# Slot numbers loaded from ScalarE's queue, the combined matrix in two tiles, and a finer-cut end, in a LoRA-and-experts kernel

## The chip, the cores and the metric

The kernel runs on one core of a Trainium2 chip. The metric is the device time of one execution in microseconds (us). Five engines matter: TensorE (PE, with its weight loads PEld), VectorE (DVE), ScalarE (ACT), GpSimd (POOL), and SyncE (SP), which only issues transfers. ScalarE and GpSimd can issue transfers as well. Sixteen DMA engines carry them all.

## The reference

Two layers, of which the first is never stored. With x of shape 8 x 512 x 2048:

```
base  = x @ W.T + b
lora  = (x @ A[slot]) @ B[slot] * 2          # slot: one number per batch, rank 16
y     = base + lora
logit = y @ route_w.T                        # 8 experts; the best one wins
h     = y @ Aexp.T                           # 8 x 16 values per token
wh    = h masked to the winning expert, times its logit
out   = x + wh @ Bexp                        # 128 x 2048
```

All arithmetic is float32. Since only logits and h are needed of y, the kernel multiplies W by the projection first: c = W.T @ [Aexp, route_w].T is a matrix of 2048 x 136, and each token then needs x @ c.

## The kernel before

**Fold (lines 352 to 386).** W comes in 16 blocks `w_0` to `w_15` of 1 MB, in four buffers, over SP's queue; the projection `pj` comes in parts, the first two over ScalarE's queue (lines 106 and 130). `chunk_w(oc)` copies a block into a regrouped form `wv`, half on ACT and half on DVE, one block ahead, and then issues the load of block oc + 4. `fold_w(oc)` does 16 matmuls per block into six PSUM tiles `pcs` (pool `ps_c`, one bank each, three chunks of c to a bank, the last bank one). After block 15 each bank is copied into `cm` (line 307), by ACT and DVE in turn. `cm` is one tile of 128 x 16 x 168: per chunk 16 columns of A for even batches, the 136 of c, and 16 columns of A for odd batches. Matmuls, copies and transfers run in the order in which they are written, on each engine; nothing is rescheduled.

**Slot numbers.** `it_i` (line 92) is the 8 slot numbers, copied from one row of DRAM into all 128 partitions by a transfer that GpSimd issues. They are used from line 165 on, for the rows of the adapter gathers.

**Turns in the fold.** The pool `ps_s` (two banks) holds short-lived results: the warm-up, the transposed adapter rows, the projected bias and adapters, and later the transposed heads `pw`.

**Steps (lines 536 to 577).** There are 32 tiles of 128 tokens and two steps per tile. A step n does, on PE, half of the `heads` of tile t (x turned, times `cm`, into a bank `ph`), `add_low` (the low-rank part), `turn_heads` (transposes `wh`), and a half of the `delta` of an earlier tile (`wh` times the experts' B, into two banks `po` of the pool `ps_o`). On DVE it does `route` (five small operations from the best logit to `wh`), `add_delta` (x plus delta, 1024 columns at once) and the turning of x. ACT and POOL regroup x ahead (`shuffle`). `ps_h` (two banks) holds `ph`; `ps_h` and `ps_o` are opened after `ps_c` is closed and take its banks. Once per batch GpSimd puts the A columns of the batch after into `cm` (line 569).

**The end.** Tile 31 is treated apart: its delta goes into single banks, `pe_h` twice in the first half, then `pe_o` (512 columns), `pe_o` (256) and `pe_s` (256); each is added and stored on its own, every second one over ScalarE's queue. Tile 30 is added and stored by halves of 1024 columns, all earlier tiles are stored whole, over SP's queue.

Of the kernel before, what the change touches and what calls it, by code (L numbers as in the profile page):

```python
# [9 lines left out]
F32 = mybir.dt.float32  # L10
# [8 lines left out]
def kernel(  # L19
# [29 lines left out]
    nc = tc.nc  # L49
    P = 128  # L50
    Q = 32
    NQ = P // Q
    B, T, D = x.shape
# [4 lines left out]
    R = ER // E  # L58
    NJ = D // P
# [3 lines left out]
    NT = B * TPB  # L63
# [4 lines left out]
    HN = D // 512 // 2  # L68
    NA = NP + R
    assert B * R == P and ER == P and DO == D and B == 2 * NQ  # L70

    const = ctx.enter_context(tc.tile_pool(name="const", bufs=1))
# [7 lines left out]
    ps_s = ctx.enter_context(tc.tile_pool(name="ps_s", bufs=2, space=bass.MemoryType.PSUM))  # L80
# [8 lines left out]


    it_i = const.tile([P, B], I32, name="it_i")
    nc.gpsimd.dma_start(out=it_i, in_=itok.to_broadcast([P, B]))
    pj = wpool.tile([P, NO, NP], F32, name="pj")
    proj_v = proj.rearrange("(c p) e -> p c e", p=P)

    def load_pj(c0, c1, eng=nc.sync):
        eng.dma_start(out=pj[:, c0:c1, :], in_=proj_v[:, c0:c1, :])
# [30 lines left out]

    nc.scalar.copy(warm_a[:, 1:2], warm_a[:, :1])
    load_pj(1, 3, nc.scalar)  # L130
    pm = ps_s.tile([P, P], F32, tag="s", name="pm")
    for _ in range(14):
        nc.tensor.matmul(pm, warm, warm, start=True, stop=True)
# [93 lines left out]

    cm = const.tile([P, NJ, NA + R], F32, name="cm")  # L230
    ad_aT = const.tile([P, NJ, P], F32, name="ad_aT")
    ad_bT = tpool.tile([P, NJ, P], F32, tag="t", name="ad_bT")
    g4 = const.tile([P, B, NP], F32, name="g4")
# [58 lines left out]
    def fold_w(oc):  # L292
        for q, (pc, (j0, n)) in enumerate(zip(pcs, groups)):
            for k in range(n):

                h, j = divmod(j0 + k, HJ)
                nc.tensor.matmul(  # L297
                    pc[:, k, :],
                    wv_tiles[oc, h][:, j, :],
                    pj[:, oc, :],  # L300
                    start=(oc == 0 and k == 0),
                    stop=(oc == NO - 1),
                    skip_group_check=True,
                )
            if oc == NO - 1:
                copy = nc.scalar.copy if q % 2 == 0 else nc.vector.tensor_copy
                copy(cm[:, j0 : j0 + n, R:NA], pc[:, :n, :])  # L307


    bp = wpool.tile([P, NP], F32, name="bp")  # L310
# [42 lines left out]
    for oc in range(NO):  # L353
        if oc + 1 < NO:
            chunk_w(oc + 1)
        fold_w(oc)
        if oc == 2:
            fill_constants()
        if oc == 4:
            load_adapters_b()  # L360
        if oc == 7:
            load_adapters_a()
        if 8 <= oc < 12:
            turn_adapters(oc - 8)
        if oc in (9, 10):
            fold_bias(range(8 * (oc - 9), 8 * (oc - 8)))
        if oc == 8:
            load_x(0)
            shuffle(0, moves[6:], nc.gpsimd.tensor_copy)
        if oc == 11:  # L370
            nc.sync.dma_start(out=fb, in_=ffn_b)
            load_x(1)
            load_x(2)
            project_bias()
        if oc in (10, 11):
            turn(ad_aT, ad_ar, oc - 10)
        if oc == 11:
            for b in range(2):
                nc.vector.tensor_copy(cm[:, :, ds(b * NA, R)], ad_aT[:, :, ts(b, R)])
        if oc == 12:  # L380
            project_adapters()
        if oc in (12, 13, 14):
            shuffle(0, moves[2 * (oc - 12) : 2 * (oc - 11)], nc.scalar.copy)
        if oc == 14:
            for h in range(2):
                turn_x(0, h)
    wctx.close()
    ps_h = ctx.enter_context(tc.tile_pool(name="ps_h", bufs=2, space=bass.MemoryType.PSUM))
    ps_o = ctx.enter_context(tc.tile_pool(name="ps_o", bufs=2, space=bass.MemoryType.PSUM))
# [4 lines left out]
    ph_tiles = {}  # L394
# [4 lines left out]
    po_tiles = {}  # L399

    def batch_of(t):
        return t // TPB

    def heads(t, j0, j1):
        s = batch_of(t) % 2
        if j0 == 0:
            ph_tiles[t] = ps_h.tile([P, 512], F32, tag="h", name=f"ph_{t}")[:, :NA]
        for j in range(j0, j1):
            nc.tensor.matmul(  # L409
                ph_tiles[t],  # L410
                xT_tiles[t][:, j, :],
                cm[:, j, ds(s * R, NA)],
                start=(j == 0),
                stop=(j == NJ - 1),
            )
# [15 lines left out]
    def add_low(t):  # L431
        b = batch_of(t)
        nc.tensor.matmul(  # L433
            ph_tiles[t][:, ds((1 - b % 2) * R, NP)],
            hT_tiles.pop(t),
            g4[:, b, :],
            start=False,
            stop=True,
            skip_group_check=True,
        )  # L440
# [21 lines left out]
    def turn_heads(t):  # L462
        pw = ps_s.tile([P, P], F32, tag="s", name=f"pw_{t}")
        nc.tensor.transpose(pw, wh_tiles.pop(t), ident)  # L464
        pw_tiles[t] = pw

    def keep_heads(t):
        whT_tiles[t] = small.tile([P, P], F32, tag="whT", name=f"whT_{t}")
        nc.scalar.copy(whT_tiles[t], pw_tiles.pop(t))  # L469

    def delta(t, h, within=None):

        c0 = h * D // 2
        if t < NT - 1:
            po = ps_o.tile([P, HN, 512], F32, tag="o", name=f"po_{t}_{h}")
            cuts = [(512, po[:, k, :]) for k in range(HN)]
            adds = [(ds(c0, D // 2), po.rearrange("p n d -> p (n d)"))]
        else:

            def bank(pool, tag, n):  # L480
                shape = [P, HN, 512] if tag == "o" else [P, 512]
                b = pool.tile(shape, F32, tag=tag, name=f"pe_{tag}")
                return n, (b[:, 0, :] if tag == "o" else b)[:, :n]

            if h == 0:
                cuts = [bank(ps_h, "h", 512), bank(ps_h, "h", 512)]
            else:
                cuts = [bank(ps_o, "o", 512), bank(ps_o, "o", 256), bank(ps_s, "s", 256)]
            adds = []
        c = c0  # L490
        for n, part in cuts:
            nc.tensor.matmul(part, whT_tiles[t], fb[:, ds(c, n)], start=True, stop=True)  # L492
            if t == NT - 1:
                adds.append((ds(c, n), part))
            c += n
            if within:
                within()
                within = None
        po_tiles[t, h] = adds

    def add_delta(t, h):
        u, k = divmod(t, TPU)
        for m, (cols, part) in enumerate(po_tiles.pop((t, h))):
            xs = x_tiles[u][:, k, cols]
            nc.vector.tensor_tensor(xs, xs, part, ALU.add)  # L505
            if t == NT - 1:
                store(t, cols, nc.scalar if m % 2 else nc.sync)
        if t == NT - 2:
            store(t, ts(h, D // 2))
        elif t < NT - 2 and h == 1:  # L510
            store(t, ds(0, D))

    def store(t, cols, eng=nc.sync):
        u, k = divmod(t, TPU)
        b, r = divmod(t, TPB)
        eng.dma_start(out=out[b, ts(r, P), cols], in_=x_tiles[u][:, k, cols])

    def piece(n):

        return divmod(n - 3, 2) if 0 <= n - 3 < 2 * NT else (-1, -1)  # L520
# [15 lines left out]
    for n in range(2 * NT + 4):  # L536
        t, h = divmod(n, 2)
        if t < NT:

            heads(t, h * HJ, h * HJ + HJ // 2)  # L540
            if n == 2:
                add_low(0)
            if n == 3:
                turn_heads(0)
            heads(t, h * HJ + HJ // 2, (h + 1) * HJ)
        if h == 0 and 0 < t <= NT:
            route(t - 1)
        tp, hp = piece(n - 1)
        if tp >= 0:
            add_delta(tp, hp)  # L550
        turn_x(t + 1, h)
        if h == 1 and 0 < t <= NT:
            keep_heads(t - 1)
        u, ms = shuffle_slot(n)
        shuffle(u, ms, nc.gpsimd.tensor_copy if n == 2 else nc.scalar.copy)
        if h == 1 and t < NT:
            turn_low(t)
        last = n in (2 * NT - 1, 2 * NT)
        if last:

            delta(*piece(n), (lambda: add_low(t)) if h else (lambda: turn_heads(t - 1)))
        elif piece(n)[0] >= 0:
            delta(*piece(n))
        if h == 1 and 0 < t < NT and not last:
            add_low(t)
        if h == 1 and t < NT:
            b, k = divmod(t, TPB)
            if k == 0 and 0 < b < B - 1:
                nc.gpsimd.tensor_copy(
                    cm[:, :, ds((b + 1) % 2 * NA, R)], ad_aT[:, :, ts(b + 1, R)]  # L570
                )
        if h == 0 and 1 < t <= NT and not last:
            turn_heads(t - 1)
        tq, hq = piece(n - 5)
        u, k = divmod(tq, TPU)
        if tq >= 0 and hq == 1 and k == TPU - 1 and u + XB < NU:
            load_x(u + XB)
# [48 lines left out]
```

## Time and profile before

| | |
|---|---|
| median of 3 runs | 334.77 us (334.49 to 335.0) |
| profiled execution | 334.58 us, its span 332.8 us |
| PE busy | 323.9 us, 97% |
| DVE, ACT, POOL busy | 233.7, 171.0, 136.3 us |
| PE clock | 0.999 of full speed |
| HBM traffic | 54.88 MB read, 33.62 MB written, 266 GB/s |

The span runs from the first to the last recorded instruction; the profiled execution's own time is 1.78 us longer. Times in the text count from the span's start. PE's busy share says that the other engines matter only where PE waits for them, and at the two ends of the span, where no PE work runs. A matmul of float32 shows as two records.

### The profile page before, as it was taken

How to read it: one execution, taken by the hardware profiler on the slowest of the kernel's cores; microseconds unless marked ns; L12 is line 12 of the kernel's file. 1: busy time of each engine (PE TensorE's matmuls, PEld its weight loads, DVE VectorE, ACT ScalarE, POOL GpSimd, SP SyncE). 2: the span in 40 equal slices, each digit the busy share in tenths (PEclk: the TensorE clock that was granted, in tenths of full speed). 3: DMA queues.
4: the chain of work that ended last, by engine and by line, in shares of the span. 5: the costliest groups of instructions: out<-in, count | busy, mean ns of one | idle time of the engine just before them, and what ended most of it. 6: DMA issues, size and time to landing. Idle time of an engine off the chain costs nothing.

```text
span 332.8 us, 5119 instructions
## 1 busy us (share of the span) xinstructions
PE 323.9 (97%) x1968; PEld 260.4 (78%) x1968; DVE 233.7 (70%) x425; ACT 171.0 (51%) x193; POOL 136.3 (41%) x143
## 2 busy tenths in 40 slices
PE   8899999999999999999999999999999999999992
PEld 8899999999777777777777777777777777777751
DVE  1133386476877877887878888888878777877753
ACT  3223236646857548565656575757566576630000
POOL 2001503989781609263535536262809081600000
PEclk9999999999999999999999999999999999999999
DMA  7999999958633394857676675849493949333336
GB/s 218 399 405 418 420 407 424 418 221 306 272 161 142 119 391 147 373 173 331 214 292 251 255 291 214 325 183 366 171 376 161 378 174 392 130 126 128 127 145 234
DMA packets 15800, 88.83 MB, mean 267 GB/s; under 512 B 1680, under 2 KB 4640, under 8 KB 5536
## 3 DMA queue, kind: packets, MB, share of 16 engines
q1 hardware_dynamic: 14544, 85.80, 65.7%
q0 software_dynamic: 528, 2.11, 2.0%
q10 hardware_dynamic: 704, 0.60, 0.6%
q8 instruction: 15, 0.25, 0.3%
q14 instruction: 9, 0.07, 0.1%
HBM read 54.88 MB, written 33.62 MB: 266 GB/s over the span
## 4 chain that ended last, share of the span: by engine, by line
PE 94%; DMA 3%; DVE 0%; ACT 0%; SPq 0%; issue 0%; DVEq 0%
PE ph L409 40%; PE po L492 32%; PE pc L297 17%; DMA w<-in_w_dram 3%; PE ph L433 2%; PE pg L342 1%; PE pw L464 1%; PE pbT L324 1%; PE pe_h L492 1%; ACT wv L286 0%; DVE x L505 0%; PE pe_o L492 0%; SPq L103 0%; DVEq L622 0%; DVE cm L307 0%
## 5 line engine op out<-in xcount | busy, mean ns | idle before, releaser
L254 POOL COPY xq<-x 32x1024 f32<-32x1024 f32 x121 | 126.2, 1043 | 118.2 <-DMA x<-in_x_dram 83.9
L254 ACT COPY xq<-x 32x1024 f32<-32x1024 f32 x135 | 140.9, 1043 | 17.9 <-DMA x<-in_x_dram 11.1
L409 PE MATMUL ph<-cm,xT 128*128 128x152 f32 x1024 | 142.6, 293 | 0.5 <-DVE cm L307 0.5
L409 PEld LDWEIGHTS ph<-cm,xT 128*128 128x128 f32 x1024 | 135.1, 190 | 9.3 <-issue 8.7
L492 PE MATMUL po<-fb,whT 128*128 128x512 f32 x248 | 116.7, 592 | 0.0
L505 DVE TENSOR_TENSOR x<-x,po 128x1024 f32<-128x1024 f32 x62 | 75.0, 1210 | 5.6 <-PE po L492 5.5
L239 DVE STREAM_TRANSPOSE xT<-xq 128x1024 f32<-128x1024 f32 x64 | 78.8, 1235 | 0.1
L492 PEld LDWEIGHTS po<-fb,whT 128*128 128x128 f32 x248 | 43.2, 190 | 29.2 <-issue 28.9
L297 PE MATMUL pc<-pj,wv 128*128 128x136 f32 x512 | 60.7, 279 | 1.5 <-ACT wv L286 1.1
L297 PEld LDWEIGHTS pc<-pj,wv 128*128 128x128 f32 x512 | 59.8, 190 | 1.9 <-ACT wv L286 1.3
L469 ACT COPY whT<-pw 128x128 f32<-128x128 f32 x32 | 8.5, 266 | 88.7 <-PE pw L464 88.7
L286 DVE COPY wv<-w 128x1024 f32<-128x1024 f32 (+1 forms) x17 | 13.5, 799 | 29.9 <-PE pc L297 16.1
L446 DVE TENSOR_REDUCE top<-ph 128x1 f32<-128x8 f32 x32 | 5.3, 167 | 37.5 <-PE ph L433 37.5
L286 ACT COPY wv<-w 128x1024 f32<-128x1024 f32 (+1 forms) x17 | 16.8, 996 | 27.9 <-DMA w<-in_w_dram 20.6
L433 PEld LDWEIGHTS ph<-g,hT 128*128 128x128 f32 x64 | 12.0, 190 | 15.0 <-issue 12.2
L452 DVE TENSOR_SCALAR rw<-rank,win,top 128x8 f32<-128x8 f32 x32 | 15.5, 484 | 1.2
L433 PE MATMUL ph<-g,hT 128*128 128x136 f32 x64 | 12.7, 280 | 0.0
L428 DVE STREAM_TRANSPOSE hT<-hls 128x128 f32<-128x128 f32 x32 | 10.0, 311 | 1.1
L173 POOL DMA_INDIRECT raw<-in_cond_b_dram,brow_i x1 | 1.0, 1032 | 23.6 <-DVE brow_i L172 23.6
L464 PEld LDWEIGHTS pw<-ident,wh 128*128 128x128 f32 x32 | 4.5, 140 | 7.7 <-issue 5.0
L454 DVE TENSOR_TENSOR wh<-ph,rw 128x128 f32<-128x128 f32 x32 | 9.3, 292 | 1.1
L464 PE MATMUL pw<-ident,wh 128*128 128x128 f32 x32 | 8.7, 273 | 0.0
(70 smaller groups left out, 81.1 us busy)
## 6 DMA issues: line engine op xcount, KB each, us to landing
x<-in_x_dram SPq DMA_DIRECT2D x32, 1024.0 KB, 8.9
out_dram<-x SPq DMA_DIRECT2D x30, 1024.0 KB, 4.8
w<-in_w_dram SPq DMA_DIRECT2D x16, 1024.0 KB, 11.8
fb<-in_ffn_b_dram SPq DMA_DIRECT2D x1, 1024.0 KB
out_dram<-x SPq DMA_DIRECT2D x2, 512.0 KB, 2.6
pj<-in_proj_dram SPq DMA_DIRECT2D x2, 272.0 KB, 11.4
out_dram<-x SPq DMA_DIRECT2D x2, 256.0 KB, 3.1
g<-g_dram SPq DMA_DIRECT2D x4, 68.0 KB, 2.5
```

Of the source, the lines that this page charges most:

```text
L239: nc.vector.transpose(dst[:, ts(h, HJ), :].rearrange("p j (g t) -> p g j t", t=Q), src.rearrange("p g (j a) -> p g j a", a=Q)[:, :, ts(h, ...
L254: copy(xq_tiles[u][ts(i, Q), :, g, :], x_tiles[u][ts(g, Q), :, ts(i, DQ)])
L286: copy(dst[:, ts(k, n)], wr[:, ds(h * HJ + k * n, n)])
L297: nc.tensor.matmul(pc[:, k, :], wv_tiles[oc, h][:, j, :], pj[:, oc, :], start=(oc == 0 and k == 0), stop=(oc == NO - 1), skip_group_check= ...
L409: nc.tensor.matmul(ph_tiles[t], xT_tiles[t][:, j, :], cm[:, j, ds(s * R, NA)], start=(j == 0), stop=(j == NJ - 1),)
L428: nc.vector.transpose(hT, h.rearrange("p g s -> p (g s)"))
L433: nc.tensor.matmul(ph_tiles[t][:, ds((1 - b % 2) * R, NP)], hT_tiles.pop(t), g4[:, b, :], start=False, stop=True, skip_group_check=True,)
L452: nc.vector.tensor_scalar(rw, rank, win, top, ALU.is_equal, ALU.mult)
L454: nc.vector.tensor_tensor(wh.rearrange("p (e r) -> p e r", r=R), ph[:, :ER].rearrange("p (e r) -> p e r", r=R), rw.unsqueeze(2).to_broadca ...
L464: nc.tensor.transpose(pw, wh_tiles.pop(t), ident)
L492: nc.tensor.matmul(part, whT_tiles[t], fb[:, ds(c, n)], start=True, stop=True)
L505: nc.vector.tensor_tensor(xs, xs, part, ALU.add)
```

## The change

The diff does the following.

- `it_i` is loaded by ScalarE, after its second part of `pj`, and no longer by GpSimd.
- `cm` becomes two tiles, one for chunks 0 to 11 (four of the six fold banks) and one for chunks 12 to 15. The A columns are placed by one copy per tile (`place_a`).
- `ph` of tile 0 is taken from `ps_s` and not from `ps_h`.
- Tile 30 is cut like tile 31: its delta goes into four single banks (`pe_o`, `pe_o`, `pe_h`, `pe_s`), each added and stored on its own by SP. The first of them is added in the step in which it is computed, ahead of `route(31)`. For tile 31 the banks are `pe_h`, `pe_o`, and then `pe_o` (512), `pe_h` (256), `pe_s` (256).

```
-    nc.gpsimd.dma_start(out=it_i, in_=itok.to_broadcast([P, B]))
...
     load_pj(1, 3, nc.scalar)
+    nc.scalar.dma_start(out=it_i, in_=itok.to_broadcast([P, B]))
...
-    cm = const.tile([P, NJ, NA + R], F32, name="cm")
+    JC = NJ * 3 // 4
+    cms = [const.tile([P, n, NA + R], F32, name=f"cm_{n}") for n in (JC, NJ - JC)]
+
+    def cm(j):
+        return cms[j // JC][:, j % JC, :]
+
+    def place_a(b, copy):
+        for k, part in enumerate(cms):
+            n = part.shape[1]
+            copy(part[:, :, ds(b % 2 * NA, R)], ad_aT[:, ds(k * JC, n), ts(b, R)])
...
-                copy(cm[:, j0 : j0 + n, R:NA], pc[:, :n, :])
+                copy(cms[j0 // JC][:, ds(j0 % JC, n), R:NA], pc[:, :n, :])
...
-                nc.vector.tensor_copy(cm[:, :, ds(b * NA, R)], ad_aT[:, :, ts(b, R)])
+                place_a(b, nc.vector.tensor_copy)
...
-            ph_tiles[t] = ps_h.tile([P, 512], F32, tag="h", name=f"ph_{t}")[:, :NA]
+            pool, tag = (ps_h, "h") if t else (ps_s, "s")
+            ph_tiles[t] = pool.tile([P, 512], F32, tag=tag, name=f"ph_{t}")[:, :NA]
...
-                cm[:, j, ds(s * R, NA)],
+                cm(j)[:, ds(s * R, NA)],
...
+    ends = {
+        (NT - 2, 0): (("o", 512), ("o", 512)),
+        (NT - 2, 1): (("h", 512), ("s", 512)),
+        (NT - 1, 0): (("h", 512), ("o", 512)),
+        (NT - 1, 1): (("o", 512), ("h", 256), ("s", 256)),
+    }
...
-        if t < NT - 1:
+        if (t, h) in ends:
+            cuts = ends[t, h]
+        else:
...
-    def add_delta(t, h):
+    def add_delta(t, h, n=None):
...
+        pieces = po_tiles[t, h]
+        po_tiles[t, h] = pieces[n:] if n else []
+        for m, (cols, part) in enumerate(pieces[:n]):
             xs = x_tiles[u][:, k, cols]
             nc.vector.tensor_tensor(xs, xs, part, ALU.add)
-            if t == NT - 1:
-                store(t, cols, nc.scalar if m % 2 else nc.sync)
-        if t == NT - 2:
-            store(t, ts(h, D // 2))
-        elif t < NT - 2 and h == 1:
-            store(t, ds(0, D))
+            if (t, h) in ends:
+                store(t, cols, nc.scalar if t == NT - 1 and m % 2 else nc.sync)
+            elif h == 1:
+                store(t, ds(0, D))
...
             delta(*piece(n), (lambda: add_low(t)) if h else (lambda: turn_heads(t - 1)))
+            if h == 1:
+                add_delta(*piece(n), 1)
...
-                nc.gpsimd.tensor_copy(
-                    cm[:, :, ds((b + 1) % 2 * NA, R)], ad_aT[:, :, ts(b + 1, R)]
-                )
+                place_a(b + 1, nc.gpsimd.tensor_copy)
```

More of the change, by code (lines that the diff above doesn't have):

```diff
@@ L469, in keep_heads, with bank @@
         nc.scalar.copy(whT_tiles[t], pw_tiles.pop(t))
+    def bank(tag, n):
+        pool, shape = {
+            "h": (ps_h, [P, 512]), "s": (ps_s, [P, 512]), "o": (ps_o, [P, HN, 512])
+        }[tag]
+        b = pool.tile(shape, F32, tag=tag, name=f"pe_{tag}")
+        return n, (b[:, 0, :] if tag == "o" else b)[:, :n]
+    ends = {
[4 more added lines that the diff above has]
+    }
     def delta(t, h, within=None):
         c0 = h * D // 2
-        if t < NT - 1:
+        if (t, h) in ends:
+            cuts = ends[t, h]
+        else:
             po = ps_o.tile([P, HN, 512], F32, tag="o", name=f"po_{t}_{h}")
             cuts = [(512, po[:, k, :]) for k in range(HN)]
[L477 to L489, printed above, removed]
-        c = c0
-        for n, part in cuts:
+            po_tiles[t, h] = [(ds(c0, D // 2), po.rearrange("p n d -> p (n d)"))]
+        c = c0
+        for cut in cuts:
+            if (t, h) in ends:
+                cut = bank(*cut)
+                po_tiles.setdefault((t, h), []).append((ds(c, cut[0]), cut[1]))
+            n, part = cut
             nc.tensor.matmul(part, whT_tiles[t], fb[:, ds(c, n)], start=True, stop=True)
-            if t == NT - 1:
-                adds.append((ds(c, n), part))
             c += n
@@ L498, in delta @@
                 within = None
-        po_tiles[t, h] = adds
-    def add_delta(t, h):
+    def add_delta(t, h, n=None):
         u, k = divmod(t, TPU)
-        for m, (cols, part) in enumerate(po_tiles.pop((t, h))):
+        pieces = po_tiles[t, h]
+        po_tiles[t, h] = pieces[n:] if n else []
+        for m, (cols, part) in enumerate(pieces[:n]):
             xs = x_tiles[u][:, k, cols]
             nc.vector.tensor_tensor(xs, xs, part, ALU.add)
-            if t == NT - 1:
-                store(t, cols, nc.scalar if m % 2 else nc.sync)
-        if t == NT - 2:
-            store(t, ts(h, D // 2))
-        elif t < NT - 2 and h == 1:
-            store(t, ds(0, D))
+            if (t, h) in ends:
+                store(t, cols, nc.scalar if t == NT - 1 and m % 2 else nc.sync)
+            elif h == 1:
+                store(t, ds(0, D))
     def store(t, cols, eng=nc.sync):
```

## The prediction

> **What bounds the kernel now.** The page's chain of work that ended last came first. By engine it reads:
>
> ```profile
> PE 94%; DMA 3%; DVE 0%; ACT 0%; SPq 0%; issue 0%; DVEq 0%
> ```
>
> TensorE (PE) works through the span, so an edit pays where PE waits, or after its last matmul. The list of waits names PE's own (total us, times, longest):
>
> ```profile
> PE pc L297 <- ACT wv L286: 1.1, 1, 1.1
> PE ph L409 <- DVE cm L307: 0.5, 1, 0.5
> ```
>
> The chain asked for in order of time (start, duration) places both:
>
> ```profile
> 1.19 9.11 DMA w<-in_w_dram
> 10.32 1.05 ACT wv L286
> 11.42 29.92 PE pc L297 x256
> ...
> 73.02 0.31 DVE cm L307
> ```
>
> PE ends its first fold at 10.28 and starts the second at 11.42, because w_1 lands only at 10.3. At the end of the fold it stops from 73.0 to 73.47 until the last bank has been copied into cm. Why is w_1 late? Busy time by stretches (length, then PE, PEld, DVE, ACT and POOL busy with counts, PE's clock, DMA share, GB/s):
>
> ```profile
> 4.00:5.00 1.00, 1.00 (x9) 1.00 (x9) 0.00 (x0) 0.00 (x0) 0.00 (x0) 1.00 0.99 411
> 5.00:6.00 1.00, 0.98 (x9) 0.79 (x8) 0.17 (x1) 0.17 (x1) 0.00 (x0) 1.00 2.03 265
> 6.00:7.00 1.00, 0.69 (x6) 0.69 (x7) 0.59 (x2) 0.97 (x2) 0.00 (x0) 1.00 0.12 34
> 8.00:9.00 1.00, 1.00 (x11) 1.00 (x10) 0.00 (x0) 0.00 (x0) 0.00 (x0) 1.00 1.00 411
> ```
>
> Traffic nearly stops between 6 and 7 us although w_1 was issued by 1.6. The DMA queues that started packets between 5.5 and 6.0 (packets, MB, share of 16 engines):
>
> ```profile
> q0 software_dynamic: 16, 0.00, 272.1%
> q1 hardware_dynamic: 4, 0.03, 18.9%
> ```
>
> 272.1% of 16 engines for 0.5 us over 16 packets is 1.36 us each: it_i, one packet per DMA engine. The packet records show 0.16 to 1.75 us for 256 B, while bias_o's 512 B packets of the same queue took 27 ns. So this small transfer holds each engine for about 1.36 us, ahead of w_1.
>
> The end, in order of time:
>
> ```profile
> 321.80 0.29 DVE L454 TENSOR_TENSOR wh<-ph,rw 128x128 f32<-128x128 f32 x1
> 322.14 0.14 PEld L464 LDWEIGHTS pw<-ident,wh 128*128 128x128 f32 x1 [0.48 <-DVE wh L454]
> 322.33 0.27 PE L464 MATMUL pw<-ident,wh 128*128 128x128 f32 x1
> 327.01 0.41 DVE L505 TENSOR_TENSOR x<-x,pe_s 128x256 f32<-128x256 f32 x1
> ```
>
> and the stretches after it:
>
> ```profile
> 323.50:324.00 0.50, 0.50 (x2) 0.19 (x1) 0.50 (x1) 0.00 (x0) 0.00 (x0) 1.00 0.00 0
> 324.00:324.50 0.50, 0.50 (x2) 0.19 (x1) 0.50 (x1) 0.00 (x0) 0.00 (x0) 1.00 0.88 360
> 328.00:329.00 1.00, 0.00 (x0) 0.00 (x0) 0.00 (x0) 0.00 (x0) 0.00 (x0) 1.00 1.06 334
> 330.00:330.50 0.50, 0.00 (x0) 0.00 (x0) 0.00 (x0) 0.00 (x0) 0.00 (x0) 1.00 0.15 23
> ```
>
> The 2 MB of the last two tiles start moving at 324.33 and keep the DMA engines full until 330.57: here bandwidth, not the last add (327.42), sets the end.
>
> **What the Trainium skill says.** "DMA: Bandwidth & Descriptors", section Queues, rings and completion order: each engine takes turns between its queues by whole packets. The trace agrees: during a 1.36 us packet of q0, q1 stands still. Same page, Issuing engines are not separate DMA queues: ScalarE's transfers interleave on the same 16 engines, so the move does not take it_i out of the way by itself. "PSUM — Partial Sum Buffer", Specifications: 8 banks of 512 FP32. Here two are in ps_s and six in ps_c, so the heads' banks lie on the fold's; the wait at 73.0 agrees.
>
> **The change, part by part**, on the clock of the profiled execution (334.58 us, span 332.8, 1.78 around it; the median of the runs, 334.77, is 0.19 above it).
>
> *1. it_i on ScalarE's queue.* POOL loses 0.72 us of issue; ident is needed only at 41, so nothing. ScalarE gains one issue of 0.40 us (its other issues), at about 1.65; its next large copy starts at 5.83. In q10's ring it_i stands behind 24 packets per engine of pj, of which the last ran until 10.5, that is after w_1. So w_1 lands about 1.36 us earlier, at 8.95; its copy (1.05) ends at 10.0, before PE is free at 10.28. Gain 11.42 - 10.28 = 1.14, less 0.02: **1.12**. It must survive: chunk 4 (copy at 21.42, ready 22.47, needed at 22.55) has 0.08 of slack. If the DMA stream moves by 1.36 it is ready at 21.11, needed at 21.43. The price of it_i on q10 is not in this trace. Low end: 8 packets an engine at 10.5 ns (the same page, Measured HBM→SBUF with SWDGE, gives that per packet; an estimate), 0.08 us. High end: the same 1.36 us, if it comes from 128 reads of one address rather than from the software queue; then w_2 and w_4 land as before, chunk 4 is ready at 22.47, and the gain is 0.05. Up to 0.3 us of cost loses nothing. I take the low end: on q10 this trace shows no 32 B packet, but those of 544 B took 28 ns and those of 4 B 9 ns, beside large ones. One more effect: as the waits of the built program show, transfers from SP and ScalarE share eight semaphores in turn, so one more shifts them. w_3's issue now waits for pj(0), landed at 5.7 (before: issued at 3.42), w_4's for pj(1,3). SP's queue stands behind, but w_2 and pj(5,8) fill the engines until past 11, so nothing.
>
> *2. c in two tiles; first heads in ps_s.* The two DVE copies at L379 become four: 1.36 us plus some 0.2, with 2 us of slack before chunk 13 is needed. Six GpSimd copies (397 ns) become twelve, with tens of us until use. The bank in ps_s is free since 62.2 (g_sb). At 73.0 the copies of groups 0, 3, 6 and 9 are done (the last at 72.67); group 12 ends at 73.29 and 15 at 73.32, needed after 12 chunks, 3.1 us later. The stop goes: **0.46**. Late next would be add_low(0): g4 landed at 77.0 for a use at 78.6; it moves with the DMA stream.
>
> *3. The last two tiles by banks.* The first bank of tile 30 is ready at 320.5; its add (0.68, as for pe_h) now precedes route(31) on DVE, so the chain from top to wh starts at 321.12 instead of 320.81 and ends at 322.40. pw follows at 322.60 instead of 322.33: PE loses 0.27, behind it pe_s, tile 31 and every add. The last matmul ends at 327.01 (326.74), the last add at 327.71 (327.42): **-0.29**. But stores begin earlier. Adds end at 321.2, 323.0, 323.6, 324.4, 325.3, 326.15, 327.0, 327.35, 327.71, and a store's packets follow 1.1 us after its add (323.22 to 324.33). 256 KB take 0.70 us at 376 GB/s and come every 0.85, so no queue builds up until the last three. The last bytes leave near 329.45 instead of 330.57: **1.1** net of the 0.29. Bounds: 0.7 (issue and small packets slower) to 1.4 (no backlog at all). The extra issues on SP cost 0.33 each, within the gaps. No bank waits: each reused one was read at least 1.5 us before.
>
> Sum: 1.12 + 0.46 + 1.1 = 2.68. 334.58 - 2.68 = 331.9 in the profiled execution, plus 0.19: **332.1 us**, 0.8% faster. Its own range is 331.6 to 332.6.
>
> **Rivals.** *The stall moves along.* If it_i is as slow on q10, part 1 gives 0.05 and the total is 1.6: 333.2. For: 128 reads of the same 32 bytes are the same there. Against: bytes of neighbours and pj went fast, and single packets alternate with w's. *The tail gives little.* If the end hangs on the last add and a fixed landing (3.1 us in the list of issues), part 3 turns into its -0.29, or 0 if DVE absorbs it: with parts 1 and 2, 333.2 to 333.5. Against: the full DMA columns until 330. *Slower.* it_i's 128 packets could each cost more than the packed ones did. Place: after w_1, ahead of w_2 to w_4; price: chunk 4 late by the excess over 1.36 us. Parts 2 and 3 give 1.6, so it decides from 1.36 + 1.6 + 0.05 = 3.0 us per engine, or 375 ns a packet, against 28 seen; at 500 ns: 335.8. *No effect* (parts 1 and 3 both fail): 334.3 to 334.7.
>
> **How the numbers follow.** The forecast 0.60; the stall moves along 0.20; tail gives little 0.10; no effect 0.05; slower 0.05. The time is the first's. 331.6 to 333.4 holds nearly all of the forecast and most of the next two. A difference of 0.2% (0.67 us) is about what can be told from none: faster 0.90, same 0.07 (no effect, and the part of the slower case that stays within), slower 0.03.
>
> **What would show it.** Right: no slice with 34 GB/s before 9 us, q0 without 256 B packets, PE's wait at L297 down to the first chunk's 0.3; ph following pc without idle time; x<-x,pe_o ahead of top at 320, pw waiting on wh by 0.2 to 0.3 longer; DMA busy from 322 with gaps, and the last bytes under 2.2 us after the last add (now 3.15). Wrong: a hole in GB/s after 9 us with chunk 2 or 4 late; a new wait of ph; a span that ends as far behind the last add as now (5.4 us; I expect 3.9).

## The result, and the profile after

The changed kernel takes 332.56 us (median of 6, 331.91 to 333.11) against 334.72: a ratio of 0.9935, 95% interval 0.9917 to 0.9952. Its profiled execution took 332.04 us with a span of 330.3, against 334.58 and 332.8. Two later comparisons of the same two kernels gave 0.9932 (0.9918 to 0.9946) and 0.9945 (0.9932 to 0.9958). The sum forecast was 2.68 us; 2.16, 2.10 and 1.85 us came.

By engine, the chain of work that ended last reads:

```profile
PE 94%; DMA 3%; SPq 0%; ACT 0%; DVE 0%; issue 0%; DVEq 0%; ACTq 0%
```

TensorE is still the bound, and a transfer still stands in the chain. In what follows, `pc` are the fold's matmuls, `ph` the heads', and a matmul counts as two records. The list of waits (total us, times, longest) names one stop in the fold:

```profile
PE pc L308 <- ACT wv L297: 0.5, 1, 0.5
```

The waits of `ph` and of block 1 are gone. The chain in order of time (start, duration) shows that this one is of another block:

```profile
2.13 11.22 DMA w<-in_w_dram
...
13.44 1.05 ACT wv L297
...
14.54 26.21 PE pc L308 x224
...
72.40 5.17 PE ph L422 x40
```

x224 of 512 records are 7 blocks of 32, and the timeline has PE at blocks 0 and 1 without a stop from 6.39 to 14.07: it now waits for **block 2**, whose copy starts at 13.44. Block 1 arrived in time (its ACT copy starts at 8.65, before at 10.32). Busy time by stretches (length, then PE, PEld, DVE, ACT and POOL with counts, PE's clock, DMA share, GB/s) gives the reason:

```profile
6.00:7.00 1.00, 1.00 (x10) 0.90 (x9) 0.67 (x2) 1.00 (x2) 0.00 (x0) 1.00 1.01 419
...
8.00:9.00 1.00, 1.00 (x11) 1.00 (x10) 0.35 (x1) 0.35 (x1) 0.00 (x0) 1.00 0.61 154
9.00:10.00 1.00, 1.00 (x11) 1.00 (x11) 0.34 (x1) 0.70 (x1) 0.00 (x0) 1.00 0.53 188
```

The hole at 6 us is filled; a new one lies at 8 to 10. Against 411 GB/s the two slices lack 480 KB, 1.17 us of traffic; the old hole (265 and 34 GB/s) lacked 523 KB, 1.27 us. The queues that started packets between 8.5 and 10.5 (packets, MB, share of 16 engines; q1 is SyncE's queue, q10 ScalarE's, q0 the software queue of GpSimd):

```profile
q1 hardware_dynamic: 129, 0.41, 56.8%
q10 hardware_dynamic: 97, 0.00, 2.4%
```

97 packets on q10 with no megabytes: 77 of them are from `it_i`'s 128 packets of 32 B. In the packet records (one per packet: queue, start, duration, size) each takes 7 to 9 ns, yet they go out from 8.11 to 10.46 us, one in 18 ns over all 16 engines, and the engines are busy neither with them nor with W (share 0.53 to 0.61).

The end, from the timeline (start, duration, engine and line, [idle before <- releaser]):

```profile
319.20 0.69 DVE L528 TENSOR_TENSOR x<-x,pe_o 128x512 f32<-128x512 f32 x1 [0.29 <-PE pe_o L515]
319.81 0.16 DVE L459 TENSOR_REDUCE top<-ph 128x1 f32<-128x8 f32 x1
...
321.13 0.14 PEld L477 LDWEIGHTS pw<-ident,wh 128*128 128x128 f32 x1 [0.77 <-DVE wh L467]
```

The first bank of tile 30 is added ahead of `top`, as forecast, and `pw` waits longer for `wh`. The last add ends at 326.28. The stretches around and after it:

```profile
326.00:327.00 1.00, 0.00 (x0) 0.00 (x0) 0.28 (x1) 0.00 (x0) 0.00 (x0) 1.00 0.91 326
327.00:328.00 1.00, 0.00 (x0) 0.00 (x0) 0.00 (x0) 0.00 (x0) 0.00 (x0) 1.00 1.00 328
328.00:329.00 1.00, 0.00 (x0) 0.00 (x0) 0.00 (x0) 0.00 (x0) 0.00 (x0) 1.00 0.12 18
```

By the packet records the last bytes leave at 328.49, 2.21 us after the last add, and the span ends at 330.27. (In the kernel before, the records put the first packet of the last 2 MB at 324.08 and the last byte at 330.39; the prediction's 324.33 and 330.57 were read about 0.2 us late.)

**Where the 2.50 us of span come from in these two executions.** `ph` of tile 0 starts at 72.40, not at 73.47, and its first 40 records take 5.17 us, not 5.41: 1.31 us up to the first delta of tile 30 (319.62 to 318.31). From there the last byte comes after 10.18 us and not 10.77: 0.59. From the last byte to the end of the span it takes 1.79 us and not 2.39: 0.60.

### The profile page after: what moved, and what is told of

It is laid out like the page before. It is cut to its first block, busy times and chain, and to the rows that moved or that the text cites. A ratio compares the mean times of both kernels' runs of the same rounds, so it can differ in the third digit from the quotient of the medians.

```text
span 330.3 us, 5132 instructions
## 1 busy us (share of the span) xinstructions
PE 324.2 (98%) x1968; PEld 260.8 (79%) x1968; DVE 234.3 (71%) x429; ACT 171.0 (52%) x193; POOL 136.7 (41%) x148
## 4 chain that ended last, share of the span: by engine, by line
PE 94%; DMA 3%; SPq 0%; ACT 0%; DVE 0%; issue 0%; DVEq 0%; ACTq 0%
PE ph L422 40%; PE po L515 31%; PE pc L308 16%; DMA w<-in_w_dram 3%; PE ph L446 2%; PE pg L353 1%; PE pw L477 1%; PE pe_o L515 1%; PE pbT L335 1%; PE pe_h L515 1%; ACT wv L297 0%; DVE x L528 0%; PE pe_s L515 0%; SPq L102 0%; SPq L96 0%
## 5 line engine op out<-in xcount | busy, mean ns | idle before, releaser
L515 PE MATMUL po<-fb,whT 128*128 128x512 f32 x240 | 112.8, 592 | 0.0
L528 DVE TENSOR_TENSOR x<-x,po 128x1024 f32<-128x1024 f32 x60 | 72.6, 1210 | 5.2 <-PE po L515 5.0
L515 PEld LDWEIGHTS po<-fb,whT 128*128 128x128 f32 x240 | 42.0, 190 | 28.7 <-issue 28.7
L297 DVE COPY wv<-w 128x1024 f32<-128x1024 f32 (+1 forms) x17 | 12.4, 737 | 31.2 <-DMA w<-in_w_dram 19.8
```

What stands on the lines that cost most here:

```text
L297: copy(dst[:, ts(k, n)], wr[:, ds(h * HJ + k * n, n)])
```

## The experiments

The theory at this point was this: the stop at the start only moved, because the price of `it_i` is 128 reads of one address and not the software queue; part 2 gave more than its wait; part 3 is limited by the DMA engines. Its rivals were that small packets as such are slow, or that the software queue was, and that the early add is what keeps part 3 small. In the table, "own rows" means that each of the 128 partitions reads its slot numbers from a row of its own in DRAM. Gains are to the median of the kernel before on the same chip (334.55 to 334.68, and 334.72 for the first result).

| kernel | median us (range, runs) | ratio, 95% interval | us gained |
|---|---|---|---|
| the change, second time | 332.58 (331.89 to 333.05, 5) | 0.9932, 0.9918 to 0.9946 | 2.10 |
| the change, third time | 332.70 (332.17 to 332.99, 5) | 0.9945, 0.9932 to 0.9958 | 1.85 |
| part 1 alone | 334.49 (333.69 to 335.10, 15) | 0.9987, 0.9979 to 0.9995 | 0.19 |
| parts 2 and 3 | 332.87 (332.68 to 333.10, 5) | 0.9949, 0.9936 to 0.9962 | 1.68 |
| change + own rows | 331.63 (331.50 to 331.71, 4) | 0.9910, 0.9895 to 0.9925 | 3.05 |
| before + own rows | 333.48 (333.02 to 333.93, 5) | 0.9961, 0.9947 to 0.9975 | 1.20 |
| change, slots late | 333.15 (333.09 to 333.45, 5) | 0.9957, 0.9943 to 0.9970 | 1.50 |
| first heads' bank alone | 333.94 (333.73 to 334.12, 12) | 0.9979, 0.9970 to 0.9987 | 0.71 |
| part 3 alone | 333.83 (333.69 to 334.15, 11) | 0.9976, 0.9967 to 0.9985 | 0.82 |
| change, add behind route | 332.82 (331.94 to 332.93, 5) | 0.9940, 0.9927 to 0.9954 | 1.83 |
| change, 8 warm-ups | 332.86 (332.11 to 334.76, 8) | 0.9950, 0.9934 to 0.9967 | 1.69 |
| own rows, 8 warm-ups | 333.01 (331.44 to 333.20, 6) | 0.9937, 0.9919 to 0.9955 | 1.54 |

### Part 1, alone and left out

Alone, it is the kernel before with the first two hunks of the diff:

```
-    nc.gpsimd.dma_start(out=it_i, in_=itok.to_broadcast([P, B]))
...
+    nc.scalar.dma_start(out=it_i, in_=itok.to_broadcast([P, B]))
```

> Only part 1: it_i on ScalarE's queue, everything else as before. My prediction's part 1 says 1.12 us faster (333.6). The first profile of the changed kernel says that the hole moves behind w_1 and leaves 0.60 (334.1). If the hole costs chunk 4 as well, 0.05 or a loss of up to 0.5 (334.7 to 335.2).

0.19 us by the median. Its chain in order of time:

```profile
17.88 1.05 ACT wv L286
18.98 22.51 PE pc L297 x192
```

PE now waits 0.57 us for block 3; before, its fold of block 3 began at about 18.90 (11.42 and two blocks of 3.74 us). The hole (197 and 221 GB/s at 8 to 10 us) is there as in the whole change, and in this execution, where the fold also started late (6.97, before 6.31), all that block 1 gained is lost again. The 15 times fall into two groups, seven from 333.69 to 334.06 and eight from 334.49 to 335.10, so part 1 alone gives 0.6 to 1.0 us or next to nothing. Which executions fall into which group was not read for this kernel; the uneven start of TensorE, below, is the likely reason.

The change without it:

> The change without its part 1 (the slot numbers stay on GpSimd's queue). If the parts are worth what each gave alone, 334.68 - 0.71 - 0.82 = 333.15 us, and part 1 inside the change is worth what lies between that and the changed kernel, about 0.2 to 0.6. If part 1 is worth the 1.12 forecast and the other parts share a gain, 333.7 or more. Its times should spread over 0.4 us at most, as those of the kernel before: PE's wait for w_1 until 11.42 us hides how long the matmuls on warm last.

332.87, against 332.70 for the whole change beside it: part 1 is worth 0.17 us by medians, and the two ranges overlap. The expected sum of the single parts (333.15) was missed by 0.28 us on the good side. Of this 0.13 is the kernel before, which took 334.55 on this chip and not 334.68; the end of the span, below, holds some of the rest. The spread of 0.4 us is as expected.

### One address, small packets, or the software queue

The same 32 B per partition on the same queue, but from 128 rows of their own in DRAM, handed over as a larger input (4 KB):

```
-    "itok": np.asarray(itok_B_0_23).reshape(1, -1)
+    "itok": np.tile(np.asarray(itok_B_0_23).reshape(1, -1), (128, 1))
...
-    nc.scalar.dma_start(out=it_i, in_=itok.to_broadcast([P, B]))
+    nc.scalar.dma_start(out=it_i, in_=itok)
```

> The changed kernel, with the slot numbers laid out in DRAM as 128 equal rows of 32 bytes, so that each partition reads its own row; queue, place and size of the transfer stay. Theory 1, one address: 128 reads of the same 32 bytes hold the DMA engines. Then the hole between 8.5 and 10 us is gone, PE waits only before the first block, and the time is 0.5 us or more below the changed kernel on the same chip. Theory 2, small rows: a row of 32 bytes costs 0.18 us an engine wherever it lies. Then the hole stays and the time is the changed kernel's within 0.2 us.

331.63 us, 0.95 less than the change on the same chip. Stretches and chain:

```profile
8.00:9.00 1.00, 1.00 (x11) 1.00 (x10) 0.34 (x1) 0.35 (x1) 0.00 (x0) 1.00 1.25 404
9.00:10.00 1.00, 1.00 (x11) 1.00 (x10) 0.35 (x1) 0.70 (x1) 0.00 (x0) 1.00 1.04 434
```

```profile
6.35 33.63 PE pc L308 x288
...
71.62 5.17 PE ph L422 x40
```

No hole, no stop in the fold. The 128 packets of 32 B go out between 8.28 and 8.77 us, at 9 ns each. Size, count and queue are those of the change; only the addresses read differ. So the cost is that of reading one address 128 times, and small packets as such are not slow. (Whether it is the address itself, or a source whose step is zero, these runs can't tell apart.)

The same rows in the kernel before, on GpSimd's queue:

> The kernel before, it_i still issued by GpSimd, but from 128 rows of its own. Theory 1, one address: its 256-byte packets take well under 0.2 us instead of 1.36, there is no hole at 6 us, w_1 lands near 8.9 and the time is 1.1 us below before (333.6). Theory 3, the software queue: the packets stay above 0.9 us and the time is that of before within 0.2 us.

```profile
5.00:6.00 1.00, 1.00 (x7) 1.00 (x6) 0.12 (x1) 0.12 (x1) 0.00 (x0) 1.00 1.01 407
6.00:7.00 1.00, 1.00 (x7) 1.00 (x7) 0.65 (x2) 1.00 (x2) 0.00 (x0) 1.00 1.02 419
```

The hole at 6 us is gone with the transfer still on the software queue; its 16 packets of 256 B take 18 ns each, where those of the broadcast took 0.16 to 1.75 us. The queue was not the cause. This one edit of the input gives 1.20 us, about what the forecast had asked of part 1 (1.12).

### The same broadcast later

The transfer is issued behind the copy of block 5, and the adapter loads that need it one block later:

```
         if oc == 4:
+            nc.scalar.dma_start(out=it_i, in_=itok.to_broadcast([P, B]))
+        if oc == 5:
             load_adapters_b()
```

> The changed kernel, but it_i is issued on ScalarE behind the copy of block 5 and used one block later; the broadcast from one address stays. If only the place of the hole matters, it lies near 25 us, where chunks 6 and 7 have over 1.5 us of slack; PE waits before no block but the first, and the time is 0.5 to 1.0 us below the changed kernel's (331.6 to 332.1). If the hole costs the fold there too, or the adapters come late for the turns at 41 us, no gain or a loss.

```profile
27.00:28.00 1.00, 1.00 (x11) 1.00 (x10) 0.00 (x0) 0.00 (x0) 0.00 (x0) 1.00 1.02 411
```

```profile
PE pbT L334 <- DMA raw<-in_cond_b_dram,brow_i: 0.6, 1, 0.6
```

Its packets go out from 26.70 to 28.91 us, as slowly as in the change (2.2 us), but W goes on at 411 GB/s. There every engine had packets of W, 8 KB each (0.32 us), to alternate with: eight packets of `it_i` per engine in 2.2 us are one in 0.28 us, about one for each packet of W. This agrees with what the Trainium skill says in "DMA: Bandwidth & Descriptors", section Queues, rings and completion order, of the turns between queues. In the change the other packets were mostly of 544 B (28 ns), and of W 7 started between 8.5 and 9.5 us instead of 50. That the long packets cover the waiting is argued from this, not shown by a run. Nothing was gained, as the second half of the expectation had it (333.15; the change took 332.58 and 332.70 on other chips): the later adapters make PE wait 0.6 us, and in the profiled execution the fold started only at 7.20.

### The first heads' bank alone

```
-            ph_tiles[t] = ps_h.tile([P, 512], F32, tag="h", name=f"ph_{t}")[:, :NA]
+            pool, tag = (ps_h, "h") if t else (ps_s, "s")
+            ph_tiles[t] = pool.tile([P, 512], F32, tag=tag, name=f"ph_{t}")[:, :NA]
```

> Half of part 2: the first heads' bank from the pool of the turns, but c in one tile as before. If the bank alone made PE wait, ph follows pc without idle time and the gain is 0.46 to 0.7 us (334.0 to 334.2). If the tile has to be split as well, the wait of 0.48 us stays and the time is that of before within 0.2.

0.71 us, with c in one tile. The chain of the kernel before, and then of this one:

```profile
73.47 5.41 PE ph L409 x40
```

```profile
72.96 5.17 PE ph L410 x40
```

The stop before `ph` is gone, and the 40 records take 5.17 us as in the change. So the bank is all of part 2's effect on that wait; splitting c was not needed for it.

The 0.24 us within the 40 records belong to the stop as well, as the starts of the single records show. Without the stop, the first `ph` starts at 72.79, 0.17 us before the last `pc` has ended (72.96): matmuls overlap, and the chain counts only what lies behind that end. Behind the stop nothing overlaps, and the second `ph` record starts 0.205 us after the first instead of 0.13. From start to start, the step from `pc` to `ph` is 0.77 us with the stop and 0.11 without. This stop thus cost TensorE about a quarter of a microsecond more than the idle time that the list of waits gives it.

### The end by banks alone, and the early add

Part 3 alone is the last hunks of the diff on the kernel before:

> Only part 3, everything else as before. My prediction: 1.1 us faster (333.6), PE 0.27 later behind pw, the last bytes under 2.2 us after the last add. The rival (a fixed landing after the last add decides): 0 to 0.3 us slower (334.7 to 335.0).

0.82 us. From the first delta of tile 30 the last byte comes after 10.20 us (before 10.77), 0.57 less, as in the change; the end of the span follows 2.24 us later (before 2.39).

The change with tile 30's first add put back behind `route(31)`:

```
-            if h == 1:
-                add_delta(*piece(n), 1)
```

> The changed kernel, but the first bank of tile 30 is added behind route(31) and not ahead of it. If the end hangs on the chain of PE and the adds, the 0.27 us of PE come back and the time falls by 0.2 to 0.3. If the DMA engines are still what is full at the end, the first store starts 1.2 us later and the time rises by 0.4 to 0.7.

332.82, beside 332.58 and 332.70 for the change on other chips: no difference that these runs show, where either theory had asked for one. Both effects are there and cancel. `pw` waits 0.48 us for `wh` again, not 0.77, and the last add ends at 326.14 instead of 326.28, counted from nearly the same start (318.34 and 318.31). But the first store of tile 30 starts at 322.27 and not at 320.79. From there the engines are full (share 0.97) and move 2.10 MB at 339 GB/s; in the change, from 322.53, they move the 1.84 MB that are left at 308 GB/s (share 0.91). The last byte leaves at 328.46, in the change at 328.49. A stretch of this kernel, to lay beside the one of the change above (326 GB/s):

```profile
326.00:327.00 1.00, 0.00 (x0) 0.00 (x0) 0.15 (x1) 0.00 (x0) 0.00 (x0) 1.00 1.05 399
```

### The start of TensorE

The change itself, run again:

> The changed kernel itself, once more, so that the three kernels beside it have it on the same chip. Its six times so far lie in two groups, 331.9 to 332.0 and 333.1. If the second group comes from a longer hole in the DMA traffic behind it_i, then a run near 333.1 shows PE idle before the second or a later block of the fold by about 1.6 us in all, where the first profile had 0.47; if it comes from the end, the span behind the last add is longer by 1.1.

> The changed kernel once more, beside the three kernels below. From the two profiles seen, 332.0 us where the 14 matmuls on warm end by 6.5 us, and 332.9 us where they end later and a chunk of w is late as well; so single times between 331.9 and 333.1, and a median within 332.0 to 332.9.

Its 16 times run from 331.89 to 333.11, those of the kernel before over 0.4 us. Of the two causes expected, neither came: in the profile at 333.05 the fold waits for one block as long as in the first (0.46 us), and the last byte stands as far before the end (1.83 and 1.79 us). What differs is how long the 14 warm-up matmuls (28 records `pm`) take; this makes 0.74 of the 1.0 us between the two profiles, and a short stop before the first `pw` the other 0.26. The chain of the kernel with the add behind route shows the long case:

```profile
1.06 6.22 PE pm L133 x28
7.28 33.51 PE pc L308 x288
```

The rate changes on the way. Between 4 and 5 us, first the change for the second time, then the change with own rows:

```profile
4.00:5.00 1.00, 1.00 (x6) 1.00 (x6) 0.00 (x0) 0.00 (x0) 0.00 (x0) 1.00 1.02 419
```

```profile
4.00:5.00 1.00, 1.00 (x10) 1.00 (x10) 0.00 (x0) 0.00 (x0) 0.00 (x0) 1.00 1.00 412
```

The trace's own clock records say when: their first entry, of the full clock, falls where the step from one `pm` record to the next goes from 213 to 112 ns. (The clock column of the stretches prints 1.00 before the first entry, too; that isn't a measurement.) Read from five executions (us):

| execution | full clock from | pm lasts | fold starts | waits in the fold for | ph starts |
|---|---|---|---|---|---|
| change | 5.34 | 5.4 | 6.39 | block 2, 0.47 | 72.40 |
| change, second | 6.71 | 6.1 | 6.96 | block 3, 0.46 | 73.14 |
| change, third | 4.24 | 4.9 | 6.43 | block 2, 0.54 | 72.50 |
| add behind route | 7.01 | 6.2 | 7.28 | none | 72.43 |
| change + own rows | 4.05 | 4.8 | 6.35 | none | 71.62 |

A late start of the fold and the hole cover each other: either leads to 72.4, and a late start with a late block to 73.1. Only with neither does `ph` start at 71.62. In the kernel before, PE's wait until 11.42 hid all this.

If the slow start is what shows, fewer warm-ups might help:

```
-    for _ in range(14):
+    for _ in range(8):
```

> The changed kernel with 8 matmuls on warm in place of 14. Theory, the slow start of PE shows where nothing else waits: at the slow rate seen (6.2 us for 14) 8 end by 4.7 us, so the fold starts when w_0 has been copied, at 6.35 us, in every run; the hole in w's stream still delays a chunk to the fold's end at 72.4; times 331.9 to 332.3, with a spread below 0.5 us. Rival, PE needs these matmuls to get fast: it idles from about 4.7 to 6.35, the first blocks of the fold run at the slow rate, and the time is equal to the changed kernel's or up to 1 us longer.

> The changed kernel with the slot numbers read as 128 rows of their own, and 8 matmuls on warm in place of 14. Theory of the slow start: fold starts at 6.35 us, no chunk late, so 331.5 us as with own rows and 14 matmuls where PE was fast early, and no run above 331.8. Rival, PE needs these matmuls: fold's first blocks slow, 332 us or more.

In the profiled executions the theory fell in this form and its rival came true, for the change even by more than the 1 us that it allowed. Stretches of the two kernels, first the change with 8 warm-ups, then own rows with 8:

```profile
7.50:8.50 1.00, 1.00 (x6) 1.00 (x5) 0.00 (x0) 0.00 (x0) 0.00 (x0) 1.00 0.94 325
```

```profile
7.50:8.50 1.00, 1.00 (x7) 1.00 (x6) 0.00 (x0) 0.00 (x0) 0.00 (x0) 0.50 1.00 336
```

Six to seven matmul records start in a microsecond of the fold, where own rows with 14 has 11. In the first, the clock records hold no full clock before 12.48 us: the warm-up ended at 4.85 without it, and after a pause of 1.7 us the fold went on slowly. In the second, the full clock came at 3.91, but was taken back from 7.33 to 10.74, after a pause of 2.0 us between warm-up and fold. `ph` starts at 74.69 and 73.35. Yet single times reach 332.11 and 331.44, so some executions seem to escape it. With own rows, where all four times with 14 lay under 331.72 (on another chip), four of six with 8 lie at 333: there the 14 matmuls earn their place. In the change itself the medians on one chip (332.86 with 8, 332.70 with 14) don't tell; the two slowest times do, 334.61 and 334.76, where the 16 with 14 end at 333.11.

## Why the prediction was right, and where it was not

The time, 332.56, lies in the range and 0.46 us above the forecast of 332.1, within the forecast's own range; "faster" was right. The mechanism held only in part: three terms of the sum were off, in both directions. That the total still came so near was partly luck: part 1 gave about 0.9 us less than forecast by the medians, and an end of the span that nobody had foreseen gave some 0.6 us back.

**Part 1, forecast 1.12, measured 0.17 to 0.19 by medians, 0.60 in the first profile of the change** (end of the fold at 72.40 instead of 73.00). Right: the hole before 9 us goes, w_1 lands early, PE does not wait for block 1. Wrong is the step that priced `it_i` on q10 at the low end, "0.08 us": it took the durations of other packets (28 ns for 544 B, 9 ns for 4 B) for the price of these. Its sum also used a figure of the Trainium skill, from "DMA: Bandwidth & Descriptors", section Measured (HBM→SBUF, 128 partitions, SWDGE, issued from GpSimd), for something else: the 10.5 ns there are the time of a whole transfer divided by all its 64 packets, and the prediction counted them for the 8 packets of one engine alone. With all 128 packets the same figure gives 1.34 us (an estimate); the runs show 2.35 us, 18 ns a packet. The high end of that bound was true, "128 reads of one address", as the two kernels with own rows show: the hole lacks 1.17 us of traffic where the old one lacked 1.27. Its consequence, a gain of 0.05, was too low: beside own rows, which starts the fold at the same time (6.35 and 6.39), the hole delays `ph` by 0.78 us, and without it 1.38 us would have been gained up to there. What the medians lack beyond that fits a late start of TensorE, which the wait of the kernel before had hidden. The sign named for being wrong, a hole in GB/s after 9 us with block 2 late, stands in the profile. So here the rival *the stall moves along* describes what happened; it asked for 333.2. The rest of the gain over it comes from that smaller loss and from the parts below.

**Part 2, forecast 0.46, measured 0.71** (the bank alone). The wait of 0.46 is gone as worked out. The step that was too small is the price of a stop: the forecast took its idle time alone, and the further 0.24 us are the overlap and the restart that it costs besides (0.77 us from start to start against 0.11). The forecast, like the change, treated the split of c as a condition, and the run with c in one tile shows that it isn't one.

**Part 3, forecast 1.1, measured 0.82 alone, and 0.59 up to the last byte in the profile of the change.** The step "256 KB take 0.70 us at 376 GB/s" failed. The prediction's own times for the 2 MB before (324.33 to 330.57) give 336 GB/s, and with the add behind `route`, where the engines are full, it is 339: 0.77 us for 256 KB. In the change the adds hand over 256 KB every 0.86 us, which is 305 GB/s, and 308 came, from 322.53 to 328.49, after a single gap of 0.9 us and without the further ones that were to be seen. So the stores keep pace with the adds until the last three, as forecast, and these then take longer. The finer cut may have a price of its own, which no run has singled out: in the packet records a row of 4 KB of tile 30 took 161 ns on average before, a row of 2 KB in the change 92, some 14% more per byte. The last bytes leave 2.21 us after the last add, where 329.45 against 327.71 had been worked out, 1.74. The adds themselves were delayed by 0.17 us and not by 0.29 (last add 7.97 us after the first delta of tile 30, before 7.80). Together, and with the last byte of before read 0.2 us late, the gain up to the last byte is 0.59 us and not 1.12. The span then ends 3.99 us after the last add, as forecast (3.9), because of something that was not: the stretch from the last byte to the end is 0.60 us shorter.

**What lies behind that 0.60.** In the five profiles with c in one tile the span ends 2.15 to 2.40 us after the last byte, in the nine with c in two tiles 1.71 to 1.83, parts 2 and 3 without part 1 among them (1.81). The instructions behind the last byte show where the time goes. About 0.19 is SyncE's: it waits for each semaphore once more, and in the change fewer of these waits are left when the last store has landed (0.50 us against 0.69). The other 0.44 is GpSimd's, between its first closing signal and the clearing of the semaphores: 0.65 us against 0.21. All five have a pause there and none of the nine, and in all five it stands just before GpSimd's 197th instruction record, also in part 1 alone, where the program is one record shorter (200, not 201) and the pause so falls one instruction nearer to the end. In the nine, GpSimd has 206 or 207 records, because each of its copies of A columns became two; the 197th is then a copy of x near 286 us, and no pause shows before it. Neither the bank alone nor the cut end alone adds a record to GpSimd (201 in both). So the 0.44 us go, as far as these runs show, with the split of c by way of the length of GpSimd's program, and that was luck. What the pause is stays open, and no run has the split alone. (The five also have one 8 KB packet of the instruction queue q14 at the very end of the span, or just after it, and the nine have none.)

**The rivals.** *The tail gives little* asked that part 3 turn into a loss or nothing; it gave 0.82 alone. *Slower* needed 3.0 us per engine; the hole is 1.17 us. *No effect* falls with the interval.

A version that beats both kernels is the change with own rows for the slot numbers, 331.63 us. It needs the slot numbers laid out 128 times in DRAM.

## What to carry to other kernels

The duration of a packet in the records is not its price: look at how long the whole transfer is spread and what GB/s do meanwhile, and don't broadcast one small row to all partitions in the middle of a stream that the compute waits for. Moving a cost to another queue leaves it in the same DMA engines; ask whether it goes, or only meets another block. And where a wait is taken away, whatever it hid (here TensorE's uneven start) becomes part of the time and of its spread.

## What was not expected of the hardware

- Reading one 32 B address 128 times takes 2.0 to 2.9 us on the software queue and 2.1 to 2.4 on ScalarE's, 15 ns or more a read, and at the start of the kernel this costs W 1.2 to 1.3 us of its traffic; 128 different rows take 0.4 to 0.6 us.
- The same 14 warm-up matmuls take 4.8 to 6.3 us from one execution to the next, because the full clock comes 3.0 to 6.1 us after the first of them. The Trainium skill states in "TensorE: Matmul & The Clock Gate", section What's actually happening, that the array starts throttled, that the warm-up is a time of about 3.4 us and no number of matmuls, and that it varies from run to run. The runs agree that it varies, but over 3.1 us, where 0.5 us each way is given there.
- After a warm-up of 8 matmuls (3.8 and 3.4 us) and a pause of 1.7 and 2.0 us, TensorE ran much of the fold's start at about 6 records in a microsecond, not 11. In one profile the full clock had not come yet (12.48 us); in the other it had come and was taken back for 3.41 us, after a pause of only 2.0.
- A stop of TensorE before `ph` cost 0.71 us where the list of waits gave it 0.46: matmuls overlap by 0.17 us when nothing stops them, and the first step after the stop takes 0.205 us, not 0.13.
- GpSimd paused for 0.31 us or more just before its 197th instruction record in all five kernels in which this record is one of the last. With five or six more records in its program the end of the span had no such pause.
